# Gate and up projections of a fused transformer block: the first sum rescaled in PSUM and the second added onto it

## The chip, the cores and the metric

The kernel runs on one core of one Trainium2 chip. The metric is the device time of one execution in microseconds (us). Engines are named as the profile names them: PE is TensorE's matrix multiply, PEld its weight load, DVE VectorE, ACT ScalarE, POOL GpSimd, SP the engine that issues the loads. [...]

## The reference

One transformer block over 2048 tokens of width 512: layer norm, causal attention with 16 heads, and beside it a gated feed-forward part whose weights are 4-bit codes with scales.

```python
x = L0_attn_hidden_states
xn = _layernorm(x, axis=-1)
x = x + _L0_attn_ref(xn, ...) + _L0_ffn_ref(xn, ...)

def _L0_ffn_ref(x, ...):
    Wg, Wu, Wd = dequant_nvfp4(gate), dequant_nvfp4(up), dequant_nvfp4(down)
    gate = jnp.einsum('th,nh->tn', xt, Wg)       # 2048 x 512 by 512 x 4096
    up = jnp.einsum('th,nh->tn', xt, Wu)
    gelu = jnp.tanh(0.7978845608028654 * (gate + 0.044715 * gate ** 3)) * gate * 0.5 + gate * 0.5
    inter = gelu * up
    out = jnp.einsum('tn,hn->th', inter, Wd)     # 4096 back to 512
```

## The kernel before

The kernel has an attention stage, an output projection (L738) and the feed-forward stage, one after the other on TensorE. The change is in the feed-forward stage. An order written out by hand holds there: each engine's instructions are issued in the order of the program's text.

**Tokens.** The normalized tokens lie in four blocks of 512 columns, named by b and taken in ORDER, 1, 2, 3, 0. [...] A block has three forms: xh (high part), and in the tile lm a scaled low part and a mixed part. They are made during the output projection: VectorE masks (L704), GpSimd subtracts (L705), VectorE forms the mixed part (L707), ScalarE scales the low part (L710), VectorE forms xh (L715).

**Weights.** The 4096 hidden features are 8 groups g of 4 columns j of 128. For each (g, j) there are three pieces: gate (m = 0), up (m = 1) and down (m = 2). A piece is loaded by SP, decoded by VectorE in five steps (code, spread, y, spread, mag; L582 to L600) and multiplied by its scales on GpSimd (L615, or L609 for down). For gate and up a second half follows: VectorE masks the high part (high, L625), GpSimd subtracts (L626), ScalarE writes two of the three parts (L627, L628) and GpSimd finishes the third (L629). These steps are spread between the products by a budget: advance(us) issues steps until their costs, given by hand, use up the stated microseconds, and the second half of a piece is issued after the fourth step of the next piece. So the place of each step in VectorE's, ScalarE's and GpSimd's queues is fixed by the program's text.

**A unit.** gate_and_up(g, j, b) is one unit of work; there are 8 x 4 x 4 = 128. It makes the gate product and the up product of 128 features for 512 tokens. products() issues 12 matmuls into two banks of PSUM: for each of four slices k of the width, two go into the first bank (high times high, and low) and one into the second (mixed). combine() makes one result of two banks: ScalarE copies the first, scaled by HIGH_SCALE, to the tile t in SBUF (L767; tg for gate, tu for up), and VectorE adds the second, scaled by MIXED_SCALE (L768). Gelu follows on ScalarE (L792), and VectorE multiplies gate and up to inter (L800).

**Downs.** After each pair of columns j the block's four token tiles are queued for the down product. down() takes one: two full 32-bit matmuls, each of two records (L816), into a bank of its own; add() adds the bank to acc on VectorE (L829). Each unit takes two of them, one behind the gate product and one behind the up product. The first five units find none queued.

All banks come from one pool of eight, in turn. A unit takes six: two for gate, two for up, two for downs.

Of the kernel before, what the change touches and what calls it, by code (L numbers as in the profile page):

```python
# [33 lines left out]
F32 = mybir.dt.float32  # L37
F32R = mybir.dt.float32r
I32 = mybir.dt.int32
AF = mybir.ActivationFunctionType  # L40
ALU = mybir.AluOpType
# [3 lines left out]
P = 128  # L45
# [5 lines left out]
TB = 512  # L51
NTB = S // TB
NK = H // P
# [8 lines left out]
SPLIT = 2.0**-12  # L62
HIGH = 0xFFFFF000 - (1 << 32)

TRUE = 2.0**14
HIGH_SCALE = (1.0 + SPLIT) * TRUE
MIXED_SCALE = -TRUE / SPLIT

ORDER = (1, 2, 3, 0)

# [4 lines left out]
def block_kernel(  # L75
# [10 lines left out]
    nc = tc.nc  # L86
# [28 lines left out]
    with (  # L115
# [25 lines left out]
        parts = [vals.tile([P, 4, P], BF16, tag=f"parts{i}", name=f"parts{i}") for i in range(4)]  # L141
# [128 lines left out]
        def score_cols(p, n, pool):  # L270

            qb, kt = steps[n]
            c0 = max(0, kt - 4 * qb) * P
            tiles = []
            for h in range(2):
                first = rows_of(p, h).start
                rows = slice(first, first + 3)
                ps = tile_of(pool, f"ps_t{p}_{n}_{h}")
                nc.tensor.matmul(  # L279
                    ps[:, c0:],  # L280
                    lhsT=ones_h[rows, :],
                    rhs=negs[p // 2, qb][rows, c0:],
                    start=True,
                    stop=False,
                )
                tiles.append(ps)
            return tiles
# [202 lines left out]
        for m in range((NP - 2) * STEPS):  # L490
# [5 lines left out]
            ps = score_cols(p, n, ps_t)  # L496
# [50 lines left out]
    def bank(name):  # L547
        return ps_f.tile([P, TB], F32, tag="f", name=name)
# [20 lines left out]
    gu, wd = {}, {}  # L569
# [67 lines left out]
    for g in range(NG):  # L637
        for j in range(0, NC, 2):
            pieces += [(g, 0, j + 1), (g, 1, j + 1), (g, 2, j + 1)]
            h, i = (g, j + 2) if j + 2 < NC else (g + 1, 0)  # L640
# [4 lines left out]
    def fetch():  # L645
        if pieces:
            staged.append((pieces[0], load_words(*pieces.pop(0))))
# [29 lines left out]
    def advance(us):  # L677

        budget[0] = min(budget[0] + us, us + 0.3)
        while budget[0] > 0:  # L680
            cost = next(work)
            if cost is None:
                return
            budget[0] -= cost

    def need(made):
        while not made():
            assert next(work) is not None
# [3 lines left out]
    lm = [lmp.tile([P, 2, NK, TB], F32R, tag=f"lm{b}", name=f"lm{b}") for b in range(NTB)]  # L692
    xh = {}

    def end(rest):
        if rest is not None:
            for _ in rest:
                pass

    def token_rest(b, k):  # L700

        x, low, mixed = xnT[b][:, k], lm[b][:, 0, k], lm[b][:, 1, k]
        high = tp.tile([P, TB], F32, tag="high", name=f"highx{b}_{k}")
        nc.vector.tensor_scalar(high.bitcast(I32), x.bitcast(I32), HIGH, None, ALU.bitwise_and)  # L704
        nc.gpsimd.tensor_tensor(low, x, high, ALU.subtract)  # L705
        yield
        nc.vector.scalar_tensor_tensor(  # L707
            mixed, high, SPLIT, low.bitcast(F32), ALU.mult, ALU.subtract
        )
        nc.scalar.activation(low, low.bitcast(F32), AF.Copy, scale=1.0 / SPLIT)  # L710

    def token_high(b, k):

        xh[b, k] = late.tile([P, TB], F32R, tag=f"aT{k}_{b}", name=f"xh{b}_{k}")
        nc.vector.scalar_tensor_tensor(  # L715
            xh[b, k], lm[b][:, 0, k].bitcast(F32), -SPLIT, xnT[b][:, k], ALU.mult, ALU.add
        )

    with tc.manual_schedule():

        wo = []
        for og in range(0, NOG, 2):
            t = gup.tile([P, 3, NK, P], F32, tag="gu", name=f"wo{og}")
            for i in range(2):
                wo.append(t[:, i].rearrange("p k o -> p (k o)"))
                nc.sync.dma_start(out=wo[og + i], in_=w_o[og + i])

        acc = [accp.tile([P, H], F32, tag=f"acc{t}", name=f"acc{t}") for t in range(NT)]
        order = [4 * b + i for b in ORDER for i in range(4)]
        for n, t in enumerate(order):  # L730
            nc.sync.dma_start(out=acc[t], in_=x[t * P : (t + 1) * P, :])
            if n in (1, 2, 3):
                fetch()
        tokens = None
        for n, t in enumerate(order):
            po = bank(f"po{t}")
            for og in range(NOG):
                nc.tensor.matmul(  # L738
                    po,
                    lhsT=aT[og][t // 4][:, (t % 4) * P : (t % 4 + 1) * P],  # L740
                    rhs=wo[og],
                    start=(og == 0),
                    stop=(og == NOG - 1),
                )
            nc.vector.tensor_tensor(acc[t], acc[t], po, ALU.add)
            end(tokens)
            tokens = token_rest(t // 4, t % 4)
            next(tokens)
            if n >= 4:
                token_high(ORDER[n // 4 - 1], n % 4)  # L750
            if n >= 3:
                advance(0.9)
        need(lambda: (0, 0, 0) in gu and (0, 1, 0) in gu)
        end(tokens)
        for k in range(NK):
            token_high(ORDER[-1], k)
        norm_stack.close()


        ip = ctx.enter_context(  # L760
            tc.tile_pool(name="inter", bufs=10, side="right", reuse_waits="tile")
        )
        ep = ctx.enter_context(tc.tile_pool(name="elem", bufs=2, side="right", reuse_waits="tile"))

        def combine(ps, dst, name):
            t = ep.tile([P, TB], F32, tag="t", name=f"t{name}")
            nc.scalar.activation(t, ps[0], AF.Copy, scale=HIGH_SCALE)  # L767
            nc.vector.scalar_tensor_tensor(dst, ps[1], MIXED_SCALE, t, ALU.mult, ALU.add)  # L768

        def products(g, m, j, b):  # L770

            ps = [bank(f"gu{g}_{m}_{j}_{b}_{i}") for i in range(2)]
            parts = gu[g, m, j]
            for k in range(NK):
                for dst, i, mov, start, stop in (
                    (ps[0], 0, xh[b, k], k == 0, False),
                    (ps[0], 1, lm[b][:, 0, k], False, k == NK - 1),
                    (ps[1], 2, lm[b][:, 1, k], k == 0, k == NK - 1),
                ):
                    nc.tensor.matmul(dst, lhsT=parts[:, i, k], rhs=mov, start=start, stop=stop)  # L780
            return ps

        inters = {}

        def gate_and_up(g, j, b):
            name = f"{g}_{j}_{b}"
            need(lambda: (g, 0, j) in gu and (g, 1, j) in gu)
            ps = products(g, 0, j, b)
            down()
            gate = ep.tile([P, TB], F32, tag="gate", name=f"gate{name}")  # L790
            combine(ps, gate, f"g{name}")
            nc.scalar.activation(gate, gate, AF.Gelu_apprx_tanh)  # L792
            advance(0.5)
            add()
            ps = products(g, 1, j, b)
            down()
            advance(0.8)
            inter = ip.tile([P, TB], F32, tag="inter", name=f"inter{name}")
            combine(ps, inter, f"u{name}")
            nc.vector.tensor_tensor(inter, gate, inter, ALU.mult)  # L800
            inters[g, j, b] = inter
            if j % 2 == 1:
                downs.extend((g, j, 4 * b + i) for i in range(4))
            add()
            advance(1.4)

        downs, adds = [], []

        def down():

            if not downs:
                return
            g, j, t = downs.pop(0)
            po = bank(f"pd{g}_{j}_{t}")
            for c in (j - 1, j):
                nc.tensor.matmul(  # L816
                    po,
                    lhsT=inters[g, c, t // 4][:, (t % 4) * P : (t % 4 + 1) * P],
                    rhs=wd[g, c],
                    start=(c == j - 1),  # L820
                    stop=(c == j),
                )
            adds.append((g, j, t, po))

        def add():
            if not adds:
                return
            g, j, t, po = adds.pop(0)
            nc.vector.scalar_tensor_tensor(acc[t], po, TRUE, acc[t], ALU.mult, ALU.add)  # L829
            if (g, j) == (NG - 1, NC - 1):  # L830
                nc.sync.dma_start(out=out[t * P : (t + 1) * P, :], in_=acc[t])

        for g in range(NG):
            for j in range(NC):
                for b in ORDER:
                    limit[0] = min(3 * (NC * g + j + 2), 3 * NC * NG)
                    gate_and_up(g, j, b)
        while downs:
            down()
            add()  # L840
# [53 lines left out]
```

## Time and profile before

| what | us |
|---|---|
| three runs | 2071.06, 2074.04, 2079.86 |
| their median | 2074.04 |
| the profiled execution's own time | 2072.73 |
| its span, first to last instruction | 2071.0 |
| attention and output projection, to the first gate matmul | about 911 |
| feed-forward stage | about 1160 |

The groups of the stage, as the page lists them: line, engine, operation, output and inputs, shapes, count, then busy us and mean ns of one, then the engine's idle time before them and what ended most of it.

```profile
L780 PE MATMUL gu<-lm,gu 128*128 128x512 f32 x2048 | 640.0, 393 | 2.3 <-DVE gate L768 1.2
L780 PE MATMUL gu<-xh,gu 128*128 128x512 f32 x1024 | 503.3, 491 | 1.2 <-ACT tg L767 1.2
L816 PE MATMUL pd<-wd,inter 128*128 128x512 f32 x1024 | 479.6, 592 | 0.6 <-DVE inter L800 0.6
L768 DVE SCALAR_TENSOR_TENSOR gate<-gu,tg 128x512 f32<-128x512 f32 x128 | 88.5, 691 | 231.5 <-ACT tg L767 231.4
L768 DVE SCALAR_TENSOR_TENSOR inter<-gu,tu 128x512 f32<-128x512 f32 x128 | 88.5, 691 | 218.8 <-ACT tu L767 218.8
L767 ACT ACTIVATE tg<-gu 128x512 f32<-128x512 f32 x128 | 76.1, 594 | 358.5 <-PE gu L780 358.5
L767 ACT ACTIVATE tu<-gu 128x512 f32<-128x512 f32 x128 | 76.3, 596 | 269.8 <-PE gu L780 269.8
```

[...]records of neighbours overlap and their mean is longer than the pace: the pace is the distance between starts. The mean of the xh group is lengthened by those that follow a down, which are recorded early. VectorE and ScalarE wait long before L767 and L768; that is idle time of engines that are not full, and it says nothing of the end by itself.

### The profile page before, as it was taken

Reading aid. Unit: us, or ns where it says so; the run is one execution under the profiler, and the core shown is the slowest. Engines: PE = TensorE matmul, PEld = TensorE weight load, DVE = VectorE, ACT = ScalarE, POOL = GpSimd, SP = SyncE. Lnnn points to the kernel's source line nnn. Section 1 sums busy time; section 2 is a strip of 40 time slices with the busy share of each in tenths; the row PEclk is TensorE's granted clock in tenths of the full one; section 3 lists DMA queues with packets and bytes.
Section 4 is the critical chain, followed back from the end, with each engine's and each line's share of the span. In section 5 each row is a group of like instructions: output and inputs, shape, how many; then the busy total and the mean of one; then the engine's idle time right before and its main releaser. Section 6 shows DMA issues by size and latency. Waiting matters only on the chain.

```text
span 2071.0 us, 28569 instructions
## 1 busy us (share of the span) xinstructions
PE 2034.8 (98%) x10560; PEld 1067.8 (52%) x10560; DVE 1174.1 (57%) x2354; ACT 740.6 (36%) x1624; POOL 451.3 (22%) x700
## 2 busy tenths in 40 slices
PE   7999999999999999999999999999999999999999
PEld 3433233332333222356666666666666666666665
DVE  5657665557555730496556465555556565555553
ACT  2113565456545577423222222222222222222221
POOL 0000021111111120353323122232313222232310
PEclk9999999999999999999999999999999999999999
DMA  3000000000000000300000000000000000000002
GB/s 122 0 11 31 1 1 1 1 1 1 1 1 1 2 2 1 97 14 26 22 16 21 16 20 20 20 20 17 22 17 18 19 20 19 20 20 16 21 3 81
DMA packets 54941, 39.63 MB, mean 19 GB/s; under 512 B 14737, under 2 KB 47505, under 8 KB 54673
## 3 DMA queue, kind: packets, MB, share of 16 engines
q1 hardware_dynamic: 54800, 37.81, 6.2%
q8 instruction: 83, 1.36, 0.3%
q14 instruction: 58, 0.47, 0.1%
HBM read 33.55 MB, written 4.19 MB: 18 GB/s over the span
## 4 chain that ended last, share of the span: by engine, by line
PE 93%; DVE 3%; ACT 2%; issue 1%; POOL 1%; DMA 0%; DVEq 0%; POOLq 0%; ACTq 0%
PE gu L780 33%; PE pd L816 21%; PE av L342 12%; PE ps_s L205 9%; PE ps_qk L161 6%; PE ps_t L279 4%; PE ps_t L294 3%; PE ps_v L444 3%; ACT prob L308 1%; PE po L738 1%; PE pm L260 0%; POOL lm L705 0%; PE ptx L433 0%; DVE highx L704 0%; DVE sums L362 0%
## 5 line engine op out<-in xcount | busy, mean ns | idle before, releaser
L780 PE MATMUL gu<-lm,gu 128*128 128x512 f32 x2048 | 640.0, 393 | 2.3 <-DVE gate L768 1.2
L780 PE MATMUL gu<-xh,gu 128*128 128x512 f32 x1024 | 503.3, 491 | 1.2 <-ACT tg L767 1.2
L816 PE MATMUL pd<-wd,inter 128*128 128x512 f32 x1024 | 479.6, 592 | 0.6 <-DVE inter L800 0.6
L780 PEld LDWEIGHTS gu<-lm,gu 128*128 128x128 f32 x2048 | 385.1, 188 | 141.3 <-issue 59.3
L229 DVE TENSOR_REDUCE tops<-ps_s 128x1 f32<-128x512 f32 x384 | 243.8, 682 | 157.3 <-PE ps_s L205 137.1
L342 PE MATMUL av<-prob,v 128*32 128x512 f32 (+3 forms) x1280 | 290.3, 542 | 3.7 <-DVE sums L362 2.8
L205 PE MATMUL ps_s<-qk,qk 32*128 32x512 f32 (+3 forms) x1280 | 291.2, 576 | 0.0
L342 PE MATMUL av<-prob,ones 128*32 128x512 f32 (+3 forms) x1280 | 290.3, 542 | 0.0
L816 PEld LDWEIGHTS pd<-wd,inter 128*128 128x128 f32 x1024 | 193.7, 189 | 149.1 <-issue 128.2
L294 PE MATMUL ps_t<-qk,qk 32*128 32x512 f32 (+3 forms) x1280 | 263.6, 535 | 0.0
L308 ACT ACTIVATE prob<-ps_t 128x512 f32<-128x512 f32 x384 | 205.8, 597 | 154.5 <-PE ps_t L294 153.2
L780 PEld LDWEIGHTS gu<-xh,gu 128*128 128x128 f32 x1024 | 192.8, 188 | 94.1 <-issue 58.6
L768 DVE SCALAR_TENSOR_TENSOR gate<-gu,tg 128x512 f32<-128x512 f32 x128 | 88.5, 691 | 231.5 <-ACT tg L767 231.4
L615 POOL TENSOR_TENSOR w<-mag,sc 128x256 f32<-128x256 f16 x128 | 98.2, 788 | 541.9 <-DVE mag L600 541.9
L768 DVE SCALAR_TENSOR_TENSOR inter<-gu,tu 128x512 f32<-128x512 f32 x128 | 88.5, 691 | 218.8 <-ACT tu L767 218.8
L767 ACT ACTIVATE tg<-gu 128x512 f32<-128x512 f32 x128 | 76.1, 594 | 358.5 <-PE gu L780 358.5
L829 DVE SCALAR_TENSOR_TENSOR acc<-pd,acc 128x512 f32<-128x512 f32 x256 | 175.4, 685 | 41.2 <-PE pd L816 41.2
L224 DVE CUSTOM_DVE_ANT_0 ps_s<-ps_s,mask_qk 128x128 f32<-128x128 f32 (+3 forms) x256 | 120.8, 517 | 100.2 <-PE ps_t L294 55.7
L767 ACT ACTIVATE tu<-gu 128x512 f32<-128x512 f32 x128 | 76.3, 596 | 269.8 <-PE gu L780 269.8
L342 PEld LDWEIGHTS av<-prob,v 128*32 128x32 f32 x1280 | 49.4, 108 | 200.9 <-issue 160.2
L319 POOL TENSOR_SCALAR_AFFINE_SELECT prob<-prob 128x256 f32<-128x256 f32 x128 | 52.0, 406 | 432.3 <-ACT prob L318 385.6
L626 POOL TENSOR_TENSOR gu<-w,high 128x512 fp32r<-128x512 f32 x64 | 85.6, 1337 | 238.7 <-DVE high L625 236.3
(75 smaller groups left out, 1965.0 us busy)
## 6 DMA issues: line engine op xcount, KB each, us to landing
pk<-packed SPq DMA_DIRECT2D x96, 128.0 KB, 2.1
sc<-scales SPq DMA_DIRECT2D x512, 8.0 KB, 1.6
x<-x SPq DMA_DIRECT2D x16, 256.0 KB, 3.5
acc<-x SPq DMA_DIRECT2D x16, 256.0 KB, 4.1
sc<-scales SPq DMA_DIRECT2D x256, 16.0 KB, 1.7
out<-acc SPq DMA_DIRECT2D x16, 256.0 KB, 2.0
wqk<-w_qk SPq DMA_DIRECT2D x4, 512.0 KB, 3.6
wv<-w_v SPq DMA_DIRECT2D x1, 1024.0 KB, 6.7
```

The source lines that it names most:

```text
L161: nc.tensor.matmul(ps, lhsT=w[:, k, which, :], rhs=xnT[b][:, k, :], start=(k == 0), stop=(k == NK - 1),)
L205: nc.tensor.matmul(ps[:, :w], lhsT=qT[p // 2, qb][rows, i * P : (i + 1) * P], rhs=kT[p // 2, c][rows, :w], start=True, stop=True,)
L224: nc.vector.tensor_tensor_reduce(ps[:, :w], ps[:, :w], mask_qk[:, TB - w :], 1.0, MASKED, ALU.add, ALU.max, top,)
L229: nc.vector.tensor_reduce(top, ps[:, :w], AX.X, ALU.max)
L294: nc.tensor.matmul(ps[:, c0:], lhsT=kT[p // 2, kt // 4][rows, (kt % 4) * P : (kt % 4 + 1) * P], rhs=qT[p // 2, qb][rows, c0:], start=False ...
L308: nc.scalar.activation(prob[:, h, :], ps, AF.Exp)
L342: nc.tensor.matmul(av[D * h : D * (h + 1), c0:], lhsT=v[kt // 4][:, kt % 4, D * head : D * (head + 1)] if h < 2 else ones, rhs=prob[:, h % ...
L767: nc.scalar.activation(t, ps[0], AF.Copy, scale=HIGH_SCALE)
L768: nc.vector.scalar_tensor_tensor(dst, ps[1], MIXED_SCALE, t, ALU.mult, ALU.add)
L780: nc.tensor.matmul(dst, lhsT=parts[:, i, k], rhs=mov, start=start, stop=stop)
L816: nc.tensor.matmul(po, lhsT=inters[g, c, t // 4][:, (t % 4) * P : (t % 4 + 1) * P], rhs=wd[g, c], start=(c == j - 1), stop=(c == j),)
L829: nc.vector.scalar_tensor_tensor(acc[t], po, TRUE, acc[t], ALU.mult, ALU.add)
```

## The change

The mixed part is no longer summed in a bank of its own. high_and_low() issues eight matmuls into one bank, and ScalarE multiplies the bank in place by HIGH_SCALE, which is now chosen so that the mixed products can be added without a factor of their own. mixed() issues the four mixed matmuls onto the same bank, none of them starting a new sum. The factor left over, SUM_SCALE, is applied where the bank is read: by gelu for the gate, and by one VectorE instruction that multiplies the up bank by SUM_SCALE and by the gelu's result. The unit's order becomes: eight gate matmuls, eight up matmuls, four mixed gate matmuls, gelu, a down, four mixed up matmuls, a down. Lines of the changed kernel stand 1 lower in the part above and 11 lower below.

```diff
-HIGH_SCALE = (1.0 + SPLIT) * TRUE
-MIXED_SCALE = -TRUE / SPLIT
+HIGH_SCALE = -(1.0 + SPLIT) * SPLIT
+SUM_SCALE = -TRUE / SPLIT
...
-        def combine(ps, dst, name):
-            t = ep.tile([P, TB], F32, tag="t", name=f"t{name}")
-            nc.scalar.activation(t, ps[0], AF.Copy, scale=HIGH_SCALE)
-            nc.vector.scalar_tensor_tensor(dst, ps[1], MIXED_SCALE, t, ALU.mult, ALU.add)
-
-        def products(g, m, j, b):
-            ps = [bank(f"gu{g}_{m}_{j}_{b}_{i}") for i in range(2)]
+        def high_and_low(g, m, j, b):
+            ps = bank(f"gu{g}_{m}_{j}_{b}")
             parts = gu[g, m, j]
             for k in range(NK):
-                for dst, i, mov, start, stop in (
-                    (ps[0], 0, xh[b, k], k == 0, False),
-                    (ps[0], 1, lm[b][:, 0, k], False, k == NK - 1),
-                    (ps[1], 2, lm[b][:, 1, k], k == 0, k == NK - 1),
-                ):
-                    nc.tensor.matmul(dst, lhsT=parts[:, i, k], rhs=mov, start=start, stop=stop)
+                for i, mov in ((0, xh[b, k]), (1, lm[b][:, 0, k])):
+                    nc.tensor.matmul(
+                        ps,
+                        lhsT=parts[:, i, k],
+                        rhs=mov,
+                        start=(k == 0 and i == 0),
+                        stop=(k == NK - 1 and i == 1),
+                    )
+            nc.scalar.activation(ps, ps, AF.Copy, scale=HIGH_SCALE)
             return ps
+
+        def mixed(g, m, j, b, ps):
+            for k in range(NK):
+                nc.tensor.matmul(
+                    ps,
+                    lhsT=gu[g, m, j][:, 2, k],
+                    rhs=lm[b][:, 1, k],
+                    start=False,
+                    stop=(k == NK - 1),
+                    skip_group_check=True,
+                )
...
-            ps = products(g, 0, j, b)
+            gate_sum = high_and_low(g, 0, j, b)
+            up_sum = high_and_low(g, 1, j, b)
+            mixed(g, 0, j, b, gate_sum)
+            gate = ep.tile([P, TB], F32, tag="gate", name=f"gate{name}")
+            nc.scalar.activation(gate, gate_sum, AF.Gelu_apprx_tanh, scale=SUM_SCALE)
             down()
-            gate = ep.tile([P, TB], F32, tag="gate", name=f"gate{name}")
-            combine(ps, gate, f"g{name}")
-            nc.scalar.activation(gate, gate, AF.Gelu_apprx_tanh)
             advance(0.5)
             add()
-            ps = products(g, 1, j, b)
+            mixed(g, 1, j, b, up_sum)
             down()
             advance(0.8)
             inter = ip.tile([P, TB], F32, tag="inter", name=f"inter{name}")
-            combine(ps, inter, f"u{name}")
-            nc.vector.tensor_tensor(inter, gate, inter, ALU.mult)
+            nc.vector.scalar_tensor_tensor(inter, up_sum, SUM_SCALE, gate, ALU.mult, ALU.mult)
```

## The prediction

> **What bounds the kernel now.** I read the page's busy shares first, then the chain of waits, then TensorE's waits in the feed-forward stage, then the timeline.
>
> ```profile
> PE 2034.8 (98%) x10560; PEld 1067.8 (52%) x10560; DVE 1174.1 (57%) x2354; ACT 740.6 (36%) x1624; POOL 451.3 (22%) x700
> PE 93%; DVE 3%; ACT 2%; issue 1%; POOL 1%; DMA 0%; DVEq 0%; POOLq 0%; ACTq 0%
> ```
>
> ```profile
> 1416.59 2.78 PE gu L780 x12
> 1419.37 1.72 PE pd L816 x4
> ```
>
> TensorE is busy and is the chain. Half a unit is twelve gate or up matmuls in 2.78 us, so 0.2315 us each, and four down records in 1.72, so 0.429 each. A unit (one call of gate_and_up) is twice that, 9.0 us. In the steady part no engine can be made faster to any use unless TensorE gets fewer or shorter matmuls. TensorE's waits in the whole feed-forward stage are these; from 953 to 2050 us there is none.
>
> ```profile
> PE gu L780 <- DVE gate L768: 1.2, 1, 1.2
> PE gu L780 <- ACT tg L767: 1.2, 1, 1.2
> PE gu L780 <- DVE inter L768: 1.0, 1, 1.0
> PE pd L816 <- DVE inter L800: 0.6, 1, 0.6
> ```
>
> All lie between 923 and 949 us, where VectorE and ScalarE catch up after the output projection. They sum to 4.0 us: that is all an ideal change of the waits could win, 0.2%.
>
> [...]code and spread (L582, L585) take 0.28 and 0.43 us, and 0.79 and 1.46 beside GpSimd.
>
> **The change, part by part.**
>
> *TensorE's work.* Per unit 24 matmuls before (two products of 4 x 3) and 24 after (4 x 2 twice, 4 x 1 twice), each with its own weights, and the same downs. The pace of 0.2315 looks set by the weight path: each load (188 ns) starts 3 ns after a matmul starts, and the next matmul some 42 ns after the load ends, whichever bank is written. It doesn't depend on the order, so 0. Bounds: matmuls that stay in their bank (xh then lm) start 233 to 235 ns apart, the others 227 to 235. If 234 were the pace of one bank, some 20 of 24 per unit x 128 x 2.5 ns is +6 us; the other way -4 us.
>
> *What goes.* VectorE loses two 0.69 combines and a 0.72 product per unit and gets one 0.69 scalar_tensor_tensor: 1.4 us x 128 = 180 us of VectorE, all beside TensorE, so 0. ScalarE keeps three instructions a unit; gelu reads PSUM (near 0.60, as tg, against 0.63). The rescale in place isn't in the trace of before: tg, PSUM to SBUF, takes 0.594; VectorE's in-place form (L224 at 512 columns) takes 0.717 against 0.682 for L229 that only reads. So 0.55 to 0.65; I take 0.594. Banks per unit fall from six to four, so the eight last two units. The downs move behind gelu's issue, but stand on TensorE behind the gate's mixed matmuls as they stood behind its product; SP issues the same loads in the same order.
>
> *The new wait, steady.* The gate's mixed matmuls now wait for ScalarE's rescale of the gate sum. It starts about 0.26 us after the last of the eight matmuls gives way (tu starts 0.49 after the start of its matmul), takes 0.594, and TensorE follows 0.05 later (tg ends 937.79, the matmul starts 937.84): 0.91. The eight up matmuls beside it last 1.85. Cover 0.94. The up rescale needs the same 0.91 and has four mixed gate matmuls and a down, 0.93 + 1.72. Free. Without downs (five first units) 0.93 only: about 0.1 each.
>
> What can be queued ahead of the gate's rescale is the weight split (L627, L628 of before). The order of the changed kernel shows one place: of four units, the second's end puts the second piece's split between its gelu and the third unit's rescale. In before that split is free, since banks stand between:
>
> ```profile
> 1421.28 0.68 DVE L829 SCALAR_TENSOR_TENSOR acc<-pd,acc 128x512 f32<-128x512 f32 x1
> 1421.88 0.28 DVE L590 TENSOR_SCALAR y<-spread 128x256 int32<-128x256 int32 x1
> 1422.19 0.29 DVE L594 TENSOR_SCALAR spread<-spread 128x256 int32<-128x256 int32 x1
> 1422.40 0.42 DVE L625 TENSOR_SCALAR high<-w 128x512 int32<-128x512 int32 x1
> ```
>
> Counted from the third unit's start (1420.92), the accumulation can start at 0.20 in the changed kernel (2036.70 against 2036.51, where VectorE is free). Then 0.60 + 0.31 + 0.21 + 0.42 by the starts above: the mask ends at 1.74. ScalarE: +0.03, 0.54 and 0.51 to the rescale, 0.594, 0.05: 3.46. TensorE wants it at 16 x 0.2315 = 3.70. Slack 0.24, of which a late weight load may use 0.1. The mask also needs the weights' multiply (L615): the second unit's gelu ends 5.5 after that unit's start, then the first piece's split 0.55, GpSimd's subtraction 1.28, two multiplies of 0.77 and VectorE's two in between 0.4, so 9.3, which is 0.3 in the third unit. So no stall: 0, but only just. If the chain is 0.5 longer, 0.3 to 0.4 us x 30 = +11 us.
>
> *The start of the stage.* Here the cover is gone. Queued ahead of the first rescale on ScalarE are the four last token scalings (L710):
>
> ```profile
> 921.15 0.63 ACT L710 ACTIVATE lm<-lm 128x512 fp32r<-128x512 f32 x1 [2.17 <-DVE lm L707]
> 921.69 0.58 ACT L767 ACTIVATE tg<-gu 128x512 f32<-128x512 f32 x1
> ...
> 922.81 0.40 PE L780 MATMUL gu<-lm,gu 128*128 128x512 f32 x1
> ...
> 924.41 0.50 PE L780 MATMUL gu<-lm,gu 128*128 128x512 f32 x1 [1.20 <-DVE gate L768]
> ```
>
> In before TensorE, which begins the stage at 911.4, runs 50 matmuls ahead of tg on eight banks. In after it can run 16: 911.4 + 3.7 = 915.1, then waits for the rescale at 921.69 + 0.58 + 0.05, so until 922.4. That is 7.3 us idle, longer than what already halves its clock, where it had idled 1.06 and 1.19 us within a few:
>
> ```profile
> 841.00:844.50 3.50, 1.31 (x12) 0.44 (x10) 0.74 (x2) 3.45 (x12) 0.81 (x2) 0.96 0.00 0
> 844.50:848.00 3.50, 3.43 (x20) 0.76 (x24) 3.46 (x5) 2.24 (x10) 1.60 (x4) 0.55 0.00 0
> ```
>
> (columns after the length: busy time of PE, PEld, DVE, ACT, POOL, then granted clock). So the eight mixed matmuls of unit 1 take about 3.7 instead of 1.85: 926.1. Unit 2, no downs: 24 x 0.2315 + 0.1 = 5.7: 931.8. Unit 3: sixteen matmuls to 935.5; its gate rescale stands behind the second split, whose chain starts at unit 2's gelu (ends 931.7): split 0.54, GpSimd's subtraction 1.28, two multiplies of 0.77 with VectorE's short ones between, 935.3; mask 0.42, split pair 1.08, rescale 0.6, 937.6. Stall 2.1. Its other eight: 939.5. Units 4 and 5: 5.65 each, 950.8; unit 6 with downs, 959.8. In before unit 7 starts at 953.6, stalls of 4.0 included. So +6.1; bounds +4 (no half clock) to +11 (a second half-clock window after unit 3's stall, and later splits).
>
> *The end.* After the last unit both have the downs of two and a half units, back to back: 0.
>
> Sum: 2072.7 (the profiled execution's time; span 2071.0) + 6.1 = 2078.8, call it 2079. The median of the runs shown, 2074.0, lies 1.3 above that execution, so +0.2 to 0.3% either way.
>
> **Rivals.** (a) Forecast: only the start costs; 2079, own range 2075 to 2085. (b) Slower: the split before the third unit's rescale stalls TensorE in each group of four units. For it: the slack is 0.24 and VectorE stands behind GpSimd near there. Against: the chain above fits. It decides from 0.24 on; at 0.5 longer, 2090. (c) Slower by pace: one-bank matmuls at 234: 2085. (d) The other side, faster: the 17 ns by which a gate matmul (231.5) exceeds a pass of the down (429/2 = 214.5) come from changing banks at every third matmul, and go for 20 of 24: 20 x 128 x 17 ns = -44 us, 2035. It passes the forecast's 6 us from about 2.4 ns per matmul on. Against: xh to lm, in one bank, is no shorter today. (e) The change doesn't do what it says, the mixed matmuls overwriting the sum: [...]the time would be that of (a).
>
> **How the numbers follow.** (a) 0.58, (b) 0.27, (c) 0.10, (d) 0.05; (e) shares (a)'s time. Predicted 2079. The range 2071 to 2095 takes (a), (c), most of (b) and the case that the start costs nothing, and leaves out (d) and a large (b). A measurement here can tell 0.5%, 10.4 us, from no change. Slower by more: (b) nearly whole, half of (c), a little of (a): 0.35. Faster by more: only (d), 0.05. Within: 0.60.
>
> **What would show it.** In the profile of after: one TensorE wait of about 7 us on ScalarE's rescale near 915, a half clock after it, one of about 2 us near 936, and none later; 9.0 us a unit; VectorE's busy time down by some 180. Wrong, if the waits on the rescale recur every fourth unit (b), or if twelve gate matmuls take other than 2.78 (c, d).

## The result

The changed kernel takes 2080.4 us (median of 11 runs) against 2073.6 for the kernel before: a ratio of 1.0033, with a 95% interval of 1.0023 to 1.0042. It is slower by about 7 us. The attention part and the output projection ahead of the feed-forward stage scatter from run to run (in the ten profiled runs the first gate matmul starts between 911.0 and 914.8 us), so sizes are taken from the stage in the traces, and the ratio says whether the whole time agrees.

The page of the changed kernel, its busy shares and its chain:

```profile
PE 2039.2 (98%) x10560; PEld 1068.5 (51%) x10560; DVE 973.7 (47%) x2098; ACT 733.6 (35%) x1624; POOL 451.9 (22%) x700
...
PE 93%; ACT 2%; DVE 2%; issue 1%; SPq 1%; POOL 1%; DMA 0%; POOLq 0%; DVEq 0%; ACTq 0%
```

VectorE has lost 200 us of its 1174, a sixth, and the kernel is slower: TensorE carries the chain with the same 93%, and VectorE's work had lain beside it. TensorE's waits from 900 us on, in the same view as before:

```profile
PE gu L785 <- ACT gu L779: 8.6, 2, 7.0
```

The four waits of before (4.0 us) are gone. One releaser is left, the rescale (L779), and it held TensorE twice in the whole stage. The timeline shows where (start, length, engine, instruction, and in brackets the idle time before it):

```profile
917.19 0.40 PE L772 MATMUL gu<-lm,gu 128*128 128x512 f32 x1
924.59 3.74 PE L785 MATMUL gu<-lm,gu 128*128 128x512 f32 x8 [7.01 <-ACT gu L779]
...
937.21 0.40 PE L772 MATMUL gu<-lm,gu 128*128 128x512 f32 x1
939.22 2.11 PE L785 MATMUL gu<-lm,gu 128*128 128x512 f32 x8 [1.61 <-ACT gu L779]
```

The same eight mixed matmuls take 3.74 us after the first wait and 2.11 after the second. The view by stretches tells why (length; then busy time of PE, PEld, DVE, ACT and POOL with counts; then the granted clock):

```profile
917.40:924.60 7.20, 0.19 (x2) 0.01 (x1) 5.49 (x11) 2.43 (x5) 3.29 (x2) 0.77 0.00 0
924.60:928.20 3.60, 3.60 (x9) 2.83 (x10) 2.84 (x7) 2.30 (x3) 0.54 (x1) 0.50 0.12 36
928.20:937.40 9.20, 9.20 (x41) 7.22 (x39) 7.04 (x13) 2.79 (x5) 5.01 (x6) 1.00 0.08 21
```

The clock fell to half during the long wait (0.77 on average over it: still 1.00 from 919.5 to 920.5 us, 0.50 from 921.5 to 924.6) and stays at half for the 3.6 us of work after it. ScalarE's own timeline says what it did meanwhile:

```profile
923.43 0.63 ACT L711 ACTIVATE lm<-lm 128x512 fp32r<-128x512 f32 x1 [2.15 <-DVE lm L708]
923.96 1.06 ACT L779 ACTIVATE gu<-gu 128x512 f32<-128x512 f32 x2
...
937.54 0.63 ACT L628 ACTIVATE gu<-high 128x512 fp32r<-128x512 f32 x1 [2.91 <-DVE high L626]
938.08 0.60 ACT L629 CAST gu<-high 128x512 fp32r<-128x512 f32 x1
938.59 1.06 ACT L779 ACTIVATE gu<-gu 128x512 f32<-128x512 f32 x2
```

ScalarE was idle 2.15 and 2.91 us just before, so it was not short of time. In its queue the rescale stood behind a token scaling, then behind a weight split, and these waited for VectorE.

The two profiled executions differ by 9.4 us in span (2080.4 and 2071.0). Of these 2.3 lie before the first gate matmul (paced from 911.4 and 913.7), in code that the change doesn't touch; this is no part of the change. From the first gate matmul to the last down matmul the kernel before takes 1155.3 us and the changed one 1162.4, so 7.1 more. The seventh unit starts 42.2 us after the first gate matmul in before and 47.7 in after: 5.4 of the 7.1 are lost in the first six units. The other 1.6 are a slower pace: a unit takes 9.000 us instead of 8.987 in 122 units.

### The profile page after: what moved, and what is told of

Read it like the earlier page. It is cut to its first block, busy times and chain, and to the rows that moved or that the text cites. A ratio compares the mean times of both kernels' runs of the same rounds, so it can differ in the third digit from the quotient of the medians.

```text
span 2080.4 us, 28154 instructions
## 1 busy us (share of the span) xinstructions
PE 2039.2 (98%) x10560; PEld 1068.5 (51%) x10560; DVE 973.7 (47%) x2098; ACT 733.6 (35%) x1624; POOL 451.9 (22%) x700
## 4 chain that ended last, share of the span: by engine, by line
PE 93%; ACT 2%; DVE 2%; issue 1%; SPq 1%; POOL 1%; DMA 0%; POOLq 0%; DVEq 0%; ACTq 0%
PE gu L772 22%; PE pd L827 21%; PE av L343 12%; PE gu L785 11%; PE ps_s L206 9%; PE ps_qk L162 6%; PE ps_t L280 4%; PE ps_t L295 3%; PE ps_v L445 3%; ACT prob L309 1%; SPq L567 1%; PE pm L261 0%; POOL lm L706 0%; PE ptx L434 0%; DVE highx L705 0%
## 5 line engine op out<-in xcount | busy, mean ns | idle before, releaser
L772 PE MATMUL gu<-xh,gu 128*128 128x512 f32 x1024 | 452.9, 442 | 0.0
L772 PE MATMUL gu<-lm,gu 128*128 128x512 f32 x1024 | 403.6, 394 | 0.0
L779 ACT ACTIVATE gu<-gu 128x512 f32<-128x512 f32 x256 | 148.6, 581 | 663.2 <-PE gu L772 663.2
L785 PE MATMUL gu<-lm,gu 128*128 128x512 f32 x1024 | 329.6, 444 | 8.6 <-ACT gu L779 8.6
L162 PE MATMUL ps_qk<-xnT,wqk 128*128 128x512 f32 x256 | 122.9, 619 | 4.1 <-ACT qk L174 2.7
L280 PE MATMUL ps_t<-neg,ones_h 3*128 3x512 bf16 (+3 forms) x640 | 117.7, 352 | 6.1 <-ACT prob L309 3.4
```

Of the source, the lines that this page charges most:

```text
L162: nc.tensor.matmul(ps, lhsT=w[:, k, which, :], rhs=xnT[b][:, k, :], start=(k == 0), stop=(k == NK - 1),)
L280: nc.tensor.matmul(ps[:, c0:], lhsT=ones_h[rows, :], rhs=negs[p // 2, qb][rows, c0:], start=True, stop=False,)
L772: nc.tensor.matmul(ps, lhsT=parts[:, i, k], rhs=mov, start=(k == 0 and i == 0), stop=(k == NK - 1 and i == 1),)
L779: nc.scalar.activation(ps, ps, AF.Copy, scale=HIGH_SCALE)
L785: nc.tensor.matmul(ps, lhsT=gu[g, m, j][:, 2, k], rhs=lm[b][:, 1, k], start=False, stop=(k == NK - 1), skip_group_check=True,)
```

## The experiments

There were two theories at first. Mine was that the loss sits at the stage's start, where TensorE could run ahead of ScalarE on eight banks and now can't, and that the steady part has cover. The rival was that the new wait costs a little in every unit, or in every fourth. The table gives the stage's length, from the first gate matmul to the last down matmul in one trace of each kernel, beside the ratio of times to the kernel before. The plain paragraphs below the excerpts of code are what was expected of each run; code left out is marked by dots.

| kernel | stage, us | against before | ratio of times, 95% interval |
|---|---|---|---|
| before | 1155.3 | | |
| changed | 1162.4 | +7.1 | 1.0033 (1.0023 to 1.0042) |
| e1_start_old | 1157.0 | +1.6 | 1.0004 (0.9996 to 1.0012) |
| e2_start_new | 1161.0 | +5.6 | 1.0027 (1.0019 to 1.0035) |
| e3_order | 1155.4 | 0.0 | 0.9998 (0.9990 to 1.0006) |
| e4_extra_copy | 1177.5 | +22.2 | 1.0107 (1.0093 to 1.0121) |
| e5_order_two_banks | 1158.4 | +3.1 | 1.0009 (1.0001 to 1.0018) |
| e6_warm | 1160.8 | +5.5 | 1.0024 (1.0014 to 1.0034) |
| e7_ahead | 1151.4 | -3.9 | 0.9972 (0.9960 to 0.9983) |
| e8_ahead_old | 1149.7 | -5.7 | 0.9968 (0.9956 to 0.9981) |

**e1_start_old and e2_start_new: the change in one part of the stage alone.**

```diff
...
+        def gate_and_up(g, j, b):
+            start = g == 0 and (j == 0 or (j == 1 and b == ORDER[0]))
+            inter = (unit_old if start else unit_new)(g, j, b)     # e1
+            inter = (unit_old if not start else unit_new)(g, j, b) # e2
```

> The first five units (those without downs) are done as before the change, two banks each, all others as in the changed kernel. If the loss lies in the start of the stage (the first rescale behind the token scalings, the half clock, the split ahead of the third unit's rescale: 5.4 us in the traces from the first gate matmul to the seventh unit) and the rest is the unit's pace (9.000 us against 8.986, 122 units: 1.7 us), the time is that of before plus 1.7: ratio 1.0008, about 2075, and TensorE's 7.0 us wait is gone. If the loss were spread over the steady units, it stays near 2080, ratio 1.003.

> The opposite: only the first five units are done as in the changed kernel, all others as before. Start theory: before plus 5.4, ratio 1.0026, about 2079, with the 7.0 and 1.6 us waits and a unit pace of 8.986. Steady theory: ratio 1.000.

Here unit_old is the unit of the kernel before, unit_new that of the changed kernel. TensorE's waits, first in e1, then in e2:

```profile
PE gu L812 <- DVE gate L800: 1.3, 1, 1.3
PE gu L812 <- ACT tg L799: 1.2, 1, 1.2
PE gu L812 <- DVE inter L800: 1.0, 1, 1.0
PE gu L787 <- ACT gu L781: 0.5, 1, 0.5
```

```profile
PE gu L787 <- ACT gu L781: 8.7, 2, 7.0
```

The parts add up: +1.6 and +5.6 come to 7.2 against the changed kernel's 7.1. Five units of 128, changed alone, bring the 7.0 us wait and most of the loss. The other 123, changed alone, bring one wait of 0.5, in the seventh unit, and the slower pace. Waits in every unit or every fourth are excluded by the steps from unit to unit in the changed kernel: all 121 from the seventh unit on are 9.000 us, third units of a group included. The first six units of e2 and of the changed kernel differ by 0.2 us, which shows how far two traces of the same start agree.

**e3_order and e5_order_two_banks: where the 13 ns per unit come from.** e3 changes only the order of the matmuls within a product. e5 has TensorE's whole order of the changed kernel, but the mixed products keep a bank of their own and are combined as before.

```diff
 # e3, in products()
-                for dst, i, mov, start, stop in (... three matmuls per k, banks 0, 0, 1 ...)
+            for k in range(NK): ... two matmuls into ps[0]
+            for k in range(NK): ... one matmul into ps[1]
 # e5, in gate_and_up()
+            high_and_low(g, 0, j, b, ps[0][0])
+            high_and_low(g, 1, j, b, ps[1][0])
+            mixed(g, 0, j, b, ps[0][1])
...
+            combine(ps[0], gate, f"g{name}")
...
+            mixed(g, 1, j, b, ps[1][1])
```

> The kernel of before with only the order of a product's twelve matmuls changed: the eight of the first bank, then the four of the second; no rescale in place, no new wait. If the pace of 9.000 comes from the order (fewer changes of bank), the unit takes 9.000 and the time is 1.7 us over before, ratio 1.0008. If it comes from the new waits or from two products side by side, the unit stays at 8.986, ratio 1.0000. If a change of bank cost 17 ns, it would be 30 us faster.

> TensorE's order of the changed kernel (eight gate, eight up, four mixed gate, down, four mixed up, down), but the mixed products in a bank of their own and combined as in the kernel before: no rescale in place and no wait of TensorE for it. If the unit's 9.000 us come from the order with two products side by side, this unit takes 9.000 too and the time is before plus 1.7 (ratio 1.0008) plus or minus a little of the start; if they come from the wait on ScalarE, 8.987 and 1.0000.

e3's unit keeps 8.987, e5's takes 9.000 (from start to start of its units, in all 121 steps). A piece of e5's chain in order of time (start, length, what):

```profile
1406.20 3.71 PE gu L773 x16
1409.91 0.93 PE gu L783 x4
1410.84 1.72 PE pd L827 x4
1412.55 0.93 PE gu L783 x4
1413.48 1.72 PE pd L827 x4
1415.20 3.71 PE gu L773 x16
```

So the slower pace belongs to the order with gate and up side by side, sixteen then four then four. Neither the wait for ScalarE nor the order within a product brings it. Both orders are streams without a gap in the trace; why one is 13 ns longer stays open.

The rest of e5's +3.1, 1.4 us, lies in the first six units. TensorE waits there 0.7 and 2.6 us, less than in before, but the clock halves again (length; TensorE's busy time first; the granted clock is the third number from the end):

```profile
934.30:937.70 3.40, 1.30 (x5) 0.67 (x4) 3.08 (x7) 0.56 (x2) 1.84 (x3) 1.00 0.05 14
937.70:941.10 3.40, 2.27 (x5) 1.82 (x6) 1.11 (x2) 2.64 (x6) 3.32 (x4) 0.50 0.16 41
```

**e4_extra_copy: how much cover the rescale has.**

```diff
+            extra = ep.tile([P, TB], F32, tag="extra", name=f"extra{name}")
+            nc.scalar.copy(extra, lm[ORDER[0]][:, 0, 0].bitcast(F32))
             gate_sum = high_and_low(g, 0, j, b)
```

> The changed kernel with one more ScalarE copy of 128x512 per unit, queued just ahead of the gate's rescale; nobody waits for its result. ScalarE is busy 35% of the span. If ScalarE's idle time covers it: no change, ratio to before 1.003. If the cover is what I worked out for the third unit of each four (0.24 us between the rescale's end and TensorE's need, because the second piece's split stands ahead), the copy's 0.51 us use it up and TensorE waits about 0.3 us in each such unit: 30 waits, about 11 us in all, ratio 1.008 to 1.009.

First the third unit of a group in the changed kernel, on ScalarE, and the matmul that waits for the rescale:

```profile
1431.69 0.60 ACT L629 CAST gu<-high 128x512 fp32r<-128x512 f32 x1
1432.20 0.58 ACT L779 ACTIVATE gu<-gu 128x512 f32<-128x512 f32 x1
```

```profile
1433.07 1.09 PE L785 MATMUL gu<-lm,gu 128*128 128x512 f32 x4
```

The rescale ends at 1432.78 and the matmul starts, unhindered, at 1433.07: with 0.05 for the signal that is a slack of 0.24. Now the same place with the copy:

```profile
1438.53 0.60 ACT L629 CAST gu<-high 128x512 fp32r<-128x512 f32 x1
1439.03 0.62 ACT L800 COPY extra<-lm 128x512 f32<-128x512 f32 x1
1439.56 1.14 ACT L779 ACTIVATE gu<-gu 128x512 f32<-128x512 f32 x2
```

```profile
1440.19 1.20 PE L785 MATMUL gu<-lm,gu 128*128 128x512 f32 x4
```

The first rescale of the pair ends at 1440.14 and the matmul follows 0.05 later. Thirty steps from unit to unit, all of third units, are 9.37 to 9.39 us instead of 9.000, so 0.385 x 30 = 11.6 us. As worked out, ScalarE, which is busy 35% of the span in the changed kernel, sets the pace where its queue is late. Of the 0.385, 0.28 lie between the starts before and after the wait, and 0.1 comes behind it: the first of the four mixed matmuls takes about 0.1 us longer to the start of the next. The view of waits lists none of these thirty, for a matmul's record, 0.40 long, covers part of the time; only the steps show them. The ratio, 1.0107, is above the 1.008 to 1.009 expected, which left out the start, where the copy cost another 3.5: the wait for the first rescale grows from 7.0 to 9.4, and the clock stays at half for one more stretch of 3.4.

**e6_warm: what the half clock costs by itself.**

```diff
+            if (g, j, b) == (0, 0, ORDER[0]):
+                warm = bank("warm")
+                for _ in range(28):
+                    nc.tensor.matmul(
+                        warm, lhsT=gu[g, 0, j][:, 0, 0], rhs=xh[b, 0], start=True, stop=True
+                    )
             mixed(g, 0, j, b, gate_sum)
```

> The changed kernel with 28 more matmuls (6.5 us) into a bank nobody reads, placed in the first unit where TensorE waits for the first rescale. If the half clock after the wait is a cost of its own, the granted clock stays full, the first unit's eight mixed matmuls take 1.9 us instead of 3.7, and the kernel is 1.85 us faster than the changed one: ratio to before 1.0024. If ScalarE and VectorE set the start anyway, the gain is eaten by a longer wait in the third unit: 1.0033.

```profile
915.99 6.69 PE L804 MATMUL warm<-xh,gu 128*128 128x512 f32 x28
923.24 2.10 PE L785 MATMUL gu<-lm,gu 128*128 128x512 f32 x8 [0.56 <-ACT gu L779]
```

Useless matmuls in the gap make the kernel faster than the changed one by 1.6 us in the stage (1160.8 against 1162.4): the eight mixed matmuls take 2.10 instead of 3.74, at full clock (1.00 granted from 916.0 to 925.2 us). The intervals of the two ratios overlap, so this rests on one trace of each; the 0.2 by which two traces of the same start differed is well below 1.6. The third unit's wait stays 1.6.

**e7_ahead and e8_ahead_old: give the run-ahead back.**

```diff
-            gate_sum = high_and_low(g, 0, j, b)
-            up_sum = high_and_low(g, 1, j, b)
+            gate_sum, up_sum = sums.pop((g, j, b), None) or pair(g, j, b)
...
+        limit[0] = 6
+        for b in ORDER:
+            sums[0, 0, b] = pair(0, 0, b)   # high_and_low of gate and of up
+        advance(3.0)
         for g in range(NG):
```

In e8 all units from the fifth on are those of the kernel before.

> The changed kernel, with the high and low sums of the first four units (64 matmuls, eight banks, 14.8 us) issued ahead of the first mixed matmul, and 3 us of the weights' decoding ahead of the first gelu; everything else the same. If the loss is lack of run-ahead at the start, TensorE reaches the first mixed matmul after the first rescale is done and doesn't wait: the seventh unit starts about 36.8 us after the first gate matmul instead of 47.7 (42.2 in before), so before minus 5.4 plus 1.7 for the pace: about 2070, ratio 0.9982. If the next weights are not decoded in time, TensorE waits at the fifth unit and the ratio is nearer 0.9995.

> As the last, but only the first four units use the rescaled sum; from the fifth on each unit is done as before the change, at 8.987 us. Start theory plus pace: 1.7 us less than the last, about 2068, ratio 0.9974. If VectorE's longer work per unit (2.1 us against 0.7) holds up the fifth and sixth unit, some of it is lost: up to 0.9985.

In e7 the four units' mixed products come as one run, without a wait:

```profile
927.10 7.44 PE L785 MATMUL gu<-lm,gu 128*128 128x512 f32 x32
938.08 2.09 PE L785 MATMUL gu<-lm,gu 128*128 128x512 f32 x8
```

From 900 us on no wait of TensorE is listed in either kernel. Both beat the kernel before, by 0.28% and 0.32%, with intervals clear of it; by the traces the stage is shorter by 3.9 and 5.7 us. With two banks for a unit's gate and up sums, eight hold the open sums of four units; with the four of before they hold two. Against the changed kernel the 11.0 us that e7 wins in the first six units are its two waits and the half clock, which are gone. Against the kernel before it is not shown that the run-ahead wins all of it: e7 and e8 also decode 3 us of weights ahead of the first gelu, and the kernel before was not run with that alone. e7 and e8 can't be told apart by their times; by the traces e8's stage is shorter by 1.7, and 1.6 of that is the pace.

The prediction put the most that the waits of before could give at 4.0 us, the sum of the four listed. e8 has the pace of before and gains 5.7. A listed wait counts from the end of the last record, and the time lost is longer. In the lines shown with the prediction the matmuls at 922.81 and 924.41 start 1.60 apart, where the pace is 0.23: 1.37 for a wait listed as 1.20, and another 0.1 before the next start. Counted so, from start to start, the four cost 5.3.

## Why the prediction was right, and where a size was off

*TensorE as the bound; VectorE's relief worth nothing.* Right: VectorE's busy time fell by 200 us (180 was worked out), and the time rose.

*The steady wait.* Right, in place and size. The slack of 0.24 in the third unit was measured as 0.24. The rescale takes 0.581, within the bounds of 0.55 to 0.65. No unit from the seventh on waits, and e4 shows that the bound was near: half a microsecond more makes it rival (b), at 0.385 per third unit where 0.3 to 0.4 was said.

*The start.* Right in each of its three parts: a first wait of 7.0 (7.3 said), the half clock (the eight mixed matmuls paced over 3.6; 3.7 said), a wait in the third unit of 1.6 (2.1 said). The sum was 6.1 and measured 5.4. The terms that were too large are the two waits, the third unit's by 0.5 and the first by 0.3. In the third unit GpSimd's two multiplies with VectorE's instructions in between were put at about 1.8 and took 1.53 together.

*The half clock.* e6 prices it at 1.6 us here. In the changed kernel it came within a wait of 7.0. In e5 it came after 3.40 us in which TensorE had been busy 1.30, and the place from which the prediction argued, where attention ends, is of this kind too, with 1.31 of 3.50 busy. How much idle time is enough isn't shown: a wait of 2.6 in e5 came with the half clock, and one of 2.6 in e3 without it (1.00 granted from 937 to 944 us).

*The pace.* Put at 0, with bounds from -4 to +6; measured +1.6. The argument that the weight path sets the pace, whatever the order, was too strong: e5 shows that the order matters by 13 ns in a unit (9.000 us against 8.987). This is not rival (c), one-bank matmuls at 234 ns: e3 also keeps eight matmuls in one bank, and its pace didn't change (8.987). Rival (d), whose 17 ns were an estimate from the pace of 231.5 ns and half of a down record's 429, is excluded by e3, which changes banks less often and gained nothing. Rival (e), mixed products that overwrite the sum, would have (a)'s time, so times don't tell them apart. That the mixed products add onto what ScalarE has written no trace shows, and the prediction took it as given; but the changed kernel's output is the block's, as it would not be if the products overwrote the sum.

So the forecast 6.1 stands against a measured 7.1 = 5.4 + 1.6, rounded. That the total came within 1 us is in part luck: the waits were overrated by 0.7 and the pace underrated by 1.6.

## What to carry to other kernels

Where the bound engine keeps its work, start with its waits, but count them from start to start: the listed 4.0 us of before were worth 5.3. The order of the same instructions moved its pace as well, by 1.6 us in the stage. The step that another engine does in the middle of a sum took away the run-ahead that separate banks gave, and this cost time (waits of 7.0 and 1.6 us, and the half clock) not where the kernel is steady but where that engine is behind, at a change of stages: look at what stands before the step in that engine's queue there. If such a step is wanted, issue enough independent sums ahead of it to last until the other engine arrives; in e7, with 64 matmuls ahead, no wait is listed.

## What had not been expected of the hardware

Two gapless orders of the same 24 matmuls and 8 down records differ by 13 ns per unit, steadily over 121 units (9.000 and 8.987). Within a unit the starts of gate and up matmuls are not even: in the changed kernel neighbours lie 226 to 238 ns apart (those behind a down, recorded 0.03 us after the start of the down's last record, left out), by their place in the order, and each place repeats to within 2 ns from unit to unit. Nothing in the trace says why.

In e5 the clock halved after a stretch of 3.40 us in which TensorE had been busy for 1.30, while a wait of 2.6 us in e3 left it at 1.00.
